# A gated delta-rule block on one core: the recurrence in two turns, joins on 128-row tiles, one PSUM pool

## The chip, the core and the metric

The kernel runs on one core of a Trainium2 chip. A core has five engines that work side by side and meet through semaphores: TensorE (matmuls, PE in the profile, with its weight loads as PEld), VectorE (DVE), ScalarE (ACT), GpSimd (POOL) and SyncE (SP), which here issues nearly all transfers (DMA). Each engine takes its instructions in the order in which they were laid down. Matmul results go to PSUM, which is used here as eight banks of 128 x 512 float32 values; everything else lies in SBUF, or in HBM when it doesn't fit. The metric is the time of one execution in microseconds. Before the change it is 4919.81 us, the median of three runs (4910.78 to 4920.14).

## The reference

Eight sequences of 512 tokens with 256 features go through one block: a normalized and modulated attention-like layer, and then a normalized and modulated feed-forward layer with experts. What matters here:

- Six modulation vectors come from a condition vector per sequence. Two of them, `ga` and `gb`, gate the two layers' results: `ga = (2*(ga >= 0) - 1) * max(|ga|, 0.25)`.
- The layer projects `h` to 16 key heads (q and k) and 32 value heads (v and z), each 128 wide. q, k and v go through a causal convolution of four taps and a SiLU. A key head serves two value heads: the kernel calls this a pair. Eight sequences by 16 pairs make 128 pairs.
- Per value head, the delta rule runs over chunks. In a chunk, `A = -(k_beta k^T * decay)` below the diagonal, `T = (I - A)^-1`, and with the state `S`:

```
v_new = T v_beta - (T (k_beta * exp(g))) S
out   = (q * exp(g)) S + tril(q k^T * decay) v_new
S     = S * exp(g_last) + (k * exp(g_last - g))^T v_new
```

- `out` is normalized, multiplied by the norm weights and by SiLU(z), and projected back to 256 features. The result, times `ga`, is added to x.
- A softmax over the mean of the tokens picks two of six experts per sequence; each is a 256-176-256 network with GELU. The weighted sum, times `gb`, is added to x.

## The kernel before, in words

The reference's chunks have 64 tokens; the kernel uses chunks of 128, which gives the same result: `NC = 4` chunks a sequence. One pair is the unit of work, and the main loop (L1075) is a software pipeline over 128 pairs. In iteration n these lists of steps are made and interleaved by `weave` (L52), which sorts all steps by their relative place in their own list; so the lists run side by side, each in its own order:

- `keys(n + LA)` with `LA = 9`: q and k of a pair nine ahead. Projection (L503), convolution (L511 on ScalarE, three L513 on VectorE), norms, the products k k^T and q k^T (L617), and the decay factors (L604, L610). The results wait in HBM (`kfar`, `qfar`, `sfar`, `m5far`, `m6far`, and the diagonal blocks in `lt`).
- one quarter of `diagonal_blocks(g)` for a group of four pairs: the inverses of the 32 x 32 diagonal blocks, by VectorE alone. A lane (partition) holds one block. Rows of 8 x 8 blocks come first, and then two joins: `join8_w`, `join8_x` and `join16_w`, `join16_x`, each a product (`mul`, such as L760 and L770) and a sum along the last axis (`red`). `minus_m` (L698) reads the matrix's block transposed.
- `join(n + 1)`: on TensorE, the 32-blocks are joined to 64 and those to 128, for eight matrices (u = 0..7: four chunks, two heads). Five steps follow one another: `w32` (L824) multiplies 128-row operands that hold two 32-blocks each, `x32` (L835) is a 32 x 32 product, `y32` (L846), `w64` (L857) and `y64` (L866) follow. Every step is eight matmuls into one PSUM bank, at output partitions that begin at 0, and then copies on ScalarE. The result is `y`, the transposed inverse.
- `values(n + 1)`: v of a pair one ahead (projection, convolution, SiLU), and `v_rows` (L890, L895), which turns them to rows.
- `recur(n)`: four chunks in a row. Per chunk, `from_state` (two matmuls `pi`, L919 and L920), `residual` (`r` on VectorE L927, `tmp` on ScalarE L932), `solve` (`u`, L941), `weigh` (`wd` on VectorE L950, `w` on ScalarE L956), `update` (`dst`, L964, and the new state on VectorE, L970 or L973), `within` (`in`, L982, `o` on VectorE, L988 or L990, and squares on ScalarE, L996). The state of one chunk is needed by the next: `pi`, `r`, `u`, `wd`, `dst`, `st` form a chain.
- `finish(n - 1)`: the norm (GpSimd), z's projection (`prz`, L1021), transposes (`ot`, L1044), the gate (`gt`, L1046), and the projection back (`op`, L1053), which is added to x.
- one side step where there is one: `before_attention` of the next sequence (L210), `after_attention` of the last one (L276: the experts), `gates` (L157).

After the steps of an iteration, the loads of the next pair's join are issued (L1110). SP issues the loads and stores in order; a load waits there until its buffer is free.

Matmuls in float32 make two records each in the profile, with a weight load each; transposes make one.

PSUM has three pools: `ps_m` with three banks (keys, values, side steps), `ps_c` with two (joins) and `ps_i` with three (recurrence and finish). A pool hands its banks out in turn, and a step that takes a bank waits for the last reader of what lay there.

`gates(b)` (L157) makes, once a sequence, 128 equal rows of the condition's SiLU, multiplies them with the weights (L166), and applies the sign and the limit of 0.25 in `sign_clip` (L147): one ScalarE copy and four VectorE instructions for each gate.

The diff touches these functions, and the main loop calls them:

Of the kernel before, what the change touches and what calls it, by code (L numbers as in the profile page):

```python
# [11 lines left out]
ALU = mybir.AluOpType  # L12
# [9 lines left out]
LA = 9  # L22
# [40 lines left out]
def adaln_block(  # L63
# [24 lines left out]
    ps_c = ctx.enter_context(tc.tile_pool(name="ps_c", bufs=2, space=PSUM))  # L88
    ps_i = ctx.enter_context(tc.tile_pool(name="ps_i", bufs=3, space=PSUM))
# [44 lines left out]
    wg6 = res.tile([P, 2, NKT, DM], F32, name="wg6")  # L134
# [12 lines left out]
    def sign_clip(dst, src, name):  # L147

        t = row.tile([P, DM], F32, name=f"sc_{name}", tag="scr", bufs=1)
        v = row.tile([P, DM], F32, name=f"sv_{name}", tag="sv", bufs=1)  # L150
        nc.scalar.copy(v, src)
        nc.vector.scalar_tensor_tensor(t, v, -1.0, v, ALU.mult, ALU.max)
        nc.vector.tensor_scalar_max(t, t, 0.25)
        nc.vector.tensor_scalar(v, v, 0.0, 2.0, ALU.is_ge, ALU.mult)
        nc.vector.scalar_tensor_tensor(dst, v, -1.0, t, ALU.add, ALU.mult)

    def gates(b):  # L157


        d = rows[b]  # L160
        sc = row.tile([P, NKT, P], F32, name=f"scr_{b}", tag="scr", bufs=1)
        nc.gpsimd.tensor_copy(sc, bc_last(silu_c[:, :, b], P))
        ps = bank(ps_m, f"gps_{b}")
        for i in range(2):
            for kt in range(NKT):
                mm(  # L166
                    ps[:, i * DM : (i + 1) * DM], sc[:, kt, :], wg6[:, i, kt, :],
                    start=kt == 0, stop=kt == NKT - 1,
                )
        for i, n in enumerate(("ga", "gb")):  # L170
            d[n] = row.tile([P, DM], F32, name=f"{n}_{b}", tag=n)
            sign_clip(d[n], ps[:, i * DM : (i + 1) * DM], f"{n}{b}")
# [37 lines left out]
    def before_attention(b):  # L210
# [63 lines left out]
        return [*norm_transposed(b, 0, 2, "a"), betas, lambda: (soft(), series()), decays]  # L274

    def after_attention(b):  # L276
# [75 lines left out]
        def hidden(t):  # L352
            if t == 0:
                f["hid"] = tiny("hid", [P, NF, SEQ])
            ps = bank(ps_m, f"f1_{b}_{t}")
            for kt in range(NKT):
                mm(  # L357
                    ps[: MF[t], :], f["s1"][:, kt, t * P : t * P + MF[t]], d["hb"][:, kt, :],
                    start=kt == 0, stop=kt == NKT - 1,
                )  # L360
            nc.scalar.activation(
                f["hid"][: MF[t], t, :], ps[: MF[t], :], AF.Gelu, bias=f["v1"][: MF[t], t : t + 1]
            )

        def result(i):
            ps = bank(ps_m, f"f2_{b}_{i}")
            for c2 in range(2):
                c = 2 * i + c2
                for t in range(NF):
                    mm(  # L370
                        ps[:, c2 * DM : (c2 + 1) * DM], f["hid"][: MF[t], t, c * P : (c + 1) * P],
# [14 lines left out]
            weigh, *[lambda t=t: hidden(t) for t in range(NF)],  # L386
            lambda: result(0), lambda: result(1),
# [3 lines left out]
    with tc.tile_pool(name="pro", bufs=1) as pro:  # L391
# [5 lines left out]
        )  # L397
        for i, col in enumerate((2 * DM, 5 * DM)):
# [19 lines left out]
        for i in (2, 6):  # L418
            nc.vector.tensor_scalar_add(modt[:, i : i + 2, :], modt[:, i : i + 2, :], 1.0)
        nc.scalar.activation(alog, alog, AF.Exp)  # L420
# [12 lines left out]
    with ExitStack() as st:  # L433
# [4 lines left out]
        keep = st.enter_context(tc.tile_pool(name="keep", bufs=LA + 3))  # L438
        far = st.enter_context(tc.tile_pool(name="far", bufs=LA + 3, space=DRAM))
# [7 lines left out]
        m5, x5, w5 = (w1b.tile([P, 8, 64], F32, name=n) for n in ("m5", "x5", "w5"))  # L447
        xw6 = w1b.tile([P, 8, 64], F32, name="xw6")
        x6, w6 = xw6[0:64], xw6[64:128]
        ysb = [w1b.tile([P, 8, P], F32, name=f"y_{i}") for i in range(2)]  # L450
        for t in (xl, yl, m5, x5, w5, xw6, *ysb):
            nc.gpsimd.memset(t, 0.0)
# [704 lines left out]
```

## Time and profile before

| what | value |
|---|---|
| median of three runs | 4919.81 us (4910.78 to 4920.14) |
| the profiled execution | 4912.86 us, its span 4911.1 us |
| TensorE busy, mean granted clock | 4569.8 us (93%), 0.965 |
| VectorE busy | 3815.8 us (78%) |
| ScalarE busy | 3120.0 us (64%) |
| GpSimd busy | 1826.3 us (37%) |
| DMA | 712.91 MB, 145 GB/s, q1 52.7% of 16 engines |
| first key projection, first recurrence | at 37.2 us, at 237.1 us |
| table loads of ScalarE for keys, values (L527) and decay (L610) | 140 and 121, 1283 ns each |

How to read it: the span is the time from the first to the last instruction of the program in one profiled execution; the run's time is a little longer. Busy time is the time in which at least one instruction of the engine runs. Matmuls overlap in their pipeline and their ends are modelled, so TensorE's busy share says little about how many results it delivers; the distance from one start to the next says more. A group of instructions is given with its line, engine, operation, output and inputs, sizes and count, then the busy time, the mean of one in ns, and after the second bar the idle time of the engine just before them, with what ended it.

### The profile page before, as it was taken

What the parts mean: (1) busy time and instruction counts of PE and PEld (TensorE: products, weight loads), DVE (VectorE), ACT (ScalarE), POOL (GpSimd) and SP (SyncE); (2) the same over time, 40 slices, a digit from 0 to 9 for tenths busy, and PEclk for the clock granted to TensorE, in tenths of its full rate; (3) what the DMA queues carried; (4) which work ended last, traced back from release to release, by engine and by line L of the source; (5) the groups of instructions that cost most, each with busy time, mean ns of one, the idle gap of its engine ahead of it and who ended that gap; (6) DMA issues with size and microseconds to landing.
All of it is one profiled execution on the core that took longest, in us unless ns stands there. A gap on an engine that the chain in (4) does not pass through costs nothing. (4 is left out here: it accounts for less than half of the span.)

```text
span 4911.1 us, 84235 instructions
## 1 busy us (share of the span) xinstructions
PE 4569.8 (93%) x27112; PEld 3262.1 (66%) x27112; DVE 3815.8 (78%) x8513; ACT 3120.0 (64%) x8899; POOL 1826.3 (37%) x1708
## 2 busy tenths in 40 slices
PE   5599999999999999999999999999999999999998
PEld 3366666666666666676666666666666666666775
DVE  4678878877878778888788887788877887878864
ACT  4566666666666666676666665666755666666553
POOL 3333434334333334334334343333333334333311
PEclk8689999999999999999999999999999999999998
DMA  5555555555555555555454555555555555556431
GB/s 154 120 142 146 145 160 150 155 145 155 151 144 155 150 151 143 141 157 159 150 158 143 146 163 147 144 157 146 160 138 145 149 151 154 140 148 158 133 107 46
DMA packets 1045671, 712.91 MB, mean 145 GB/s; under 512 B 661105, under 2 KB 909809, under 8 KB 1045233
## 3 DMA queue, kind: packets, MB, share of 16 engines
q1 hardware_dynamic: 1044416, 705.69, 52.7%
q8 instruction: 219, 3.59, 0.3%
q14 instruction: 220, 1.79, 0.1%
q10 hardware_dynamic: 816, 1.84, 0.1%
HBM read 459.27 MB, written 247.99 MB: 144 GB/s over the span
## 5 line engine op out<-in xcount | busy, mean ns | idle before, releaser
L513 DVE SCALAR_TENSOR_TENSOR cvv<-prv,cw,cvv 128x511 f32<-128x511 f32 (+2 forms) x768 | 560.5, 742 | 19.8 <-ACT cvv L511 18.3
L996 ACT ACTIVATE jo<-o 128x128 f32<-128x128 f32 x1024 | 304.5, 298 | 386.1 <-DVE o L990 350.9
L1031 POOL TENSOR_TENSOR msq<-msq,mhalf 128x8 f32<-128x8 f32 x128 | 223.3, 1744 | 876.6 <-DVE msq L1030 758.4
L1053 PE MATMUL op<-wo,gt 128*128 128x256 f32 x2048 | 504.9, 385 | 28.4 <-DVE gt L1046 21.8
L1021 PE MATMUL prz<-ha,wz 128*128 128x512 f32 x1024 | 496.7, 607 | 14.8 <-DMA wz<-in_dram 12.0
L637 POOL TENSOR_TENSOR mta<-mta,dca 128x512 f32<-128x512 f32 x256 | 326.3, 1275 | 466.6 <-DVE mta L626 429.4
L503 PE MATMUL prv<-ha,wv 128*128 128x512 f32 x1024 | 492.9, 603 | 4.9 <-DVE cvk L513 4.7
L604 ACT ACTIVATE dca<-gb,G 128x128 f32<-128x128 f32 x1024 | 334.8, 392 | 239.5 <-DMA sfar<-dca 179.8
L1053 PEld LDWEIGHTS op<-wo,gt 128*128 128x128 f32 x2048 | 370.6, 191 | 101.5 <-DVE gt L1046 37.4
L956 ACT ACTIVATE w<-u,br 128x128 f32<-128x128 f32 x1024 | 320.5, 361 | 164.3 <-DVE wd L950 130.0
L567 POOL TENSOR_TENSOR nrmk<-nrmk,half 128x4 f32<-128x4 f32 x128 | 140.9, 1101 | 741.3 <-ACT jk L563 727.5
L639 POOL TENSOR_TENSOR dca<-qkm,dca 128x256 f32<-128x256 f32 x512 | 387.6, 778 | 18.7 <-DVE qkm L631 0.6
L982 PEld LDWEIGHTS in<-w,s 128*128 128x128 f32 x2048 | 312.4, 197 | 92.7 <-issue 55.5
L982 PE MATMUL in<-w,s 128*128 128x128 f32 x2048 | 337.4, 287 | 4.3 <-ACT w L956 4.3
L617 PE MATMUL kk<-kqa 128*128 128x256 f32 x1024 | 314.2, 419 | 26.0 <-ACT kqa L527 14.6
L964 PE MATMUL dst<-wd,kr 128*128 128x256 f32 x768 | 265.7, 428 | 77.0 <-DVE wd L950 52.2
L513 DVE SCALAR_TENSOR_TENSOR cvk<-prk,cw,cvk 128x511 f32<-128x511 f32 (+2 forms) x384 | 285.8, 744 | 60.8 <-ACT cvk L511 57.8
L555 POOL TENSOR_TENSOR sq<-kqa 128x512 f32<-128x512 f32 x128 | 135.8, 1061 | 530.3 <-ACT kqa L527 530.3
L513 DVE SCALAR_TENSOR_TENSOR cvq<-prq,cw,cvq 128x511 f32<-128x511 f32 (+2 forms) x384 | 285.6, 744 | 40.6 <-ACT cvq L511 39.0
L503 PEld LDWEIGHTS prv<-ha,wv 128*128 128x128 f32 x1024 | 187.4, 192 | 182.8 <-issue 169.7
L941 PEld LDWEIGHTS u<-r,y 128*128 128x128 f32 x1536 | 235.7, 192 | 106.4 <-issue 51.9
L941 PE MATMUL u<-r,y 128*128 128x128 f32 x1536 | 291.2, 293 | 15.9 <-DVE r L927 15.1
(218 smaller groups left out, 11310.3 us busy)
## 6 DMA issues: line engine op xcount, KB each, us to landing
gb<-gfar SPq DMA_DIRECT2D x128, 512.0 KB
qfar<-kqa SPq DMA_DIRECT2D x128, 512.0 KB
kq<-qfar SPq DMA_DIRECT2D x128, 512.0 KB
sfar<-dca SPq DMA_DIRECT2D x256, 256.0 KB
s<-sfar SPq DMA_DIRECT2D x128, 512.0 KB
wk<-in_dram SPq DMA_DIRECT2D x256, 128.0 KB
wv<-in_dram SPq DMA_DIRECT2D x128, 256.0 KB
wz<-in_dram SPq DMA_DIRECT2D x128, 256.0 KB
```

Source lines behind the costliest of these rows:

```text
L503: mm(ps, d[wname][:, kt, j * P : (j + 1) * P], hT[:, kt, :], start=kt == 0, stop=kt == NKT - 1,)
L513: nc.vector.scalar_tensor_tensor(a[:, s:], ps[:, : SEQ - s], cw[:, ch, 3 - s : 4 - s], a[:, s:], ALU.mult, ALU.add,)
L604: nc.scalar.activation(dc[:, c, h, :], d["gb"][:, 2 * gr + c, h * P : (h + 1) * P], AF.Relu, bias=rw["G"][:, 2 * gr + c, k : k + 1], scale ...
L617: mm(ps[:, c2 * 2 * P : (c2 + 1) * 2 * P], d["kqa"][:, c, 0, :], d["kqa"][:, c].rearrange("p k i -> p (k i)"), start=True, stop=True,)
L637: nc.gpsimd.tensor_tensor(mt, mt, dc.rearrange("p c h i -> p (c h) i"), ALU.mult)
L639: nc.gpsimd.tensor_tensor(dc[:, c], bc_mid(d[f"qkm{gr}"][:, c, :], 2), dc[:, c], ALU.mult)
L941: mm(ps[:, h * P : (h + 1) * P], d["y"][:, 2 * c + h, :], r[:, h, :], start=True, stop=True,)
L956: nc.scalar.activation(w[:, h, :], ps[:, h * P : (h + 1) * P], AF.Copy, scale=d["br2"][:, c, h : h + 1],)
L982: mm(ps[:, h * P : (h + 1) * P], d["s"][:, 2 * c + h, :], cur["w"][:, h, :], start=True, stop=True,)
L996: nc.scalar.activation(junk, d["o"][:, c, h, :], AF.Square, accum_out=d["msq"][:, c, h : h + 1])
L1021: mm(ps, d["wz"][:, kt, h * P : (h + 1) * P], hT[:, kt, :], start=kt == 0, stop=kt == NKT - 1,)
L1053: mm(ps[:, k * DM : (k + 1) * DM], gt[h][:, c * P : (c + 1) * P], d["wo"][:, h, :], start=h == 0, stop=h == 1,)
```

## The change

The change has seven parts.

1. The recurrence takes two turns. `recur(n, 0)` does chunks 0 and 1 of pair n, and in the same iteration `recur(n - 1, 1)` does chunks 2 and 3 of the pair before. `finish` follows one iteration later, for pair n - 2. Values for `o`, `vr` and the loads of `kq`, `kr` and `s` are now kept in halves; the parts of `kq` and `kr` that are never used are no longer loaded. The gate's result is written over z.
2. Joins of two pairs go side by side: `join_w` multiplies the 32-join of the newer pair and the 64-join of the older one, in turn, and `join_y` ends both. All operands have 128 rows, with zeros where there is nothing, and one pair's results go to output partitions 0 to 63, the other's to 64 to 127 (in `join_y`, the product that was `x32` goes to 64 to 127). Their matmuls are laid down with high priority. Loads are issued in two parts: `join_diagonal` after an iteration, `join_corner` in `join_w`. There are four `y` tiles in place of two.
3. `ps_c` is gone; `ps_i` has five banks, for joins too.
4. The gates of all sequences are made once, in the prologue, on eight rows, and kept in HBM; `gates(b)` only loads them, spread to 128 partitions.
5. `LA` is 10 in place of 9. The five small tiles that a pair keeps until its turn are one tile, `kept`.
6. In `diagonal_blocks` the order of each join's two products is changed, so that no operand is read transposed.
7. The experts' hidden layer and result go by halves of 256 tokens; side steps of a sequence are put together (three steps before attention) and begin two iterations later.

```diff
-LA = 9
+LA = 10
...
-    ps_c = ctx.enter_context(tc.tile_pool(name="ps_c", bufs=2, space=PSUM))
-    ps_i = ctx.enter_context(tc.tile_pool(name="ps_i", bufs=3, space=PSUM))
+    ps_i = ctx.enter_context(tc.tile_pool(name="ps_i", bufs=5, space=PSUM))
...
     def gates(b):
-        d = rows[b]
-        sc = row.tile([P, NKT, P], F32, name=f"scr_{b}", tag="scr", bufs=1)
-        nc.gpsimd.tensor_copy(sc, bc_last(silu_c[:, :, b], P))
...
-            sign_clip(d[n], ps[:, i * DM : (i + 1) * DM], f"{n}{b}")
+        t = row.tile([P, 2 * DM], F32, name=f"gates_{b}", tag="gates")
+        nc.sync.dma_start(t, gates_far[b : b + 1, :].to_broadcast([P, 2 * DM]))
+        rows[b]["ga"], rows[b]["gb"] = t[:, :DM], t[:, DM:]
...
-            weigh, *[lambda t=t: hidden(t) for t in range(NF)],
-            lambda: result(0), lambda: result(1),
+            weigh, lambda: (hidden(0, 0), hidden(0, 1)), lambda: hidden(0, 2), lambda: result(0),
+            lambda: (hidden(1, 0), hidden(1, 1)), lambda: hidden(1, 2), lambda: result(1),
...
-            def join16_w(c, n, b):
-
-                pr = e["pr"].rearrange("p (c a b) -> p c a b", c=n, a=16)
+            def join16_w(a, n, w):
+
+                pr = e["pr"].rearrange("p (a b r) -> p a b r", a=n, b=16)
                 mul(
-                    pr, bc(minus_m(16, b, 16, 16 - b), 1, n), bc(part(yl, c, b, n, 16 - b), 2, 16),
+                    pr, bc(part(xl, 16 + a, 16, n, w), 2, 16), bc(part(e["t"], 0, 16, 16, w), 1, n),
                     ALU.mult,
                 )
...
+        def join_w(old, new):
+
+            p6 = bank(ps_i, f"w6_{old}") if old is not None else None
+            p5 = bank(ps_i, f"w5_{new}") if new is not None else None
+            with tc.high_priority(offset=1000):
+                for u in range(8):
+                    us = slice(64 * u, 64 * u + 64)
+                    if new is not None:
+                        mm(p5[:64, us], m5[:, u, :], x5[:, u, :], start=True, stop=True)
+                    if old is not None:
+                        mm(p6[64:, us], m6[:, u, :], x6[:, u, :], start=True, stop=True)
+            if old is not None:
+                nc.scalar.copy(w6[64:128], of_u(p6, 64)[64:128])
+            if new is not None:
+                v = of_u(p5, 64)
                 nc.scalar.copy(w5[32:64, :, 0:32], v[0:32, :, 0:32])
                 nc.scalar.copy(w5[96:128, :, 32:64], v[32:64, :, 32:64])
+                join_corner(new)
+
+        def join_y(old, new):
...
+            with tc.high_priority(offset=1000):
                 for u in range(8):
+                    us = slice(64 * u, 64 * u + 64)
+                    if new is not None:
+                        mm(p5[:64, us], w5[:, u, :], halves(y5[:, u, :]), start=True, stop=True)
+                        mm(
+                            p5[64:, 32 * u : 32 * u + 32], y5[:, u, 0:64], w5[:, u, 0:32],
+                            start=True, stop=True,
+                        )
+                    if old is not None:
+                        mm(p6[:64, us], w6[:, u, :], y6[:, u, 64:128], start=True, stop=True)
+            if old is not None:
+                nc.scalar.copy(y6[0:64, :, 64:128], of_u(p6, 64)[0:64])
+            if new is not None:
+                v = of_u(p5, 64)
+                nc.scalar.copy(x6[32:64, :, 0:32], of_u(p5, 32)[96:128])
+                nc.scalar.copy(y5[0:32, :, 32:64], v[0:32, :, 0:32])
+                nc.scalar.copy(y5[64:96, :, 96:128], v[32:64, :, 32:64])
...
-            for c in range(NC):
+            for c in (2 * half, 2 * half + 1):
                 if c:
                     steps.append(lambda c=c: from_state(c))
                     steps.append(lambda c=c: residual(c))
...
-                gt[h] = w1b.tile([P, SEQ], F32, name=f"gt{h}_{n}", tag=f"gt{h}")
+                gt[h] = d[f"z{h}"]
...
             if 0 <= m <= last:
-                sj = loaded.pop(m)
-                load, sv = values(m)
-                load()
-                streams += [sj, sv]
+                load_half(m, 0)
+                streams.append(values(m))
             if 0 <= n <= last:
-                streams.append(recur(n))
-            if 0 < n:
-                streams.append(finish(n - 1))
+                load_half(n, 1)
+            old = m if 0 <= m <= last else None
+            new = m + 1 if 0 <= m + 1 <= last else None
+            if old is not None or new is not None:
+                streams.append([
+                    lambda old=old, new=new: join_w(old, new), lambda old=old, new=new: join_y(old, new),
+                ])
+            if 0 <= n <= last:
+                streams.append(recur(n, 0))
+            if 0 <= n - 1 <= last:
+                streams.append(recur(n - 1, 1))
+            if 0 <= n - 2 <= last:
+                streams.append(finish(n - 2))
             weave(*streams, side.pop(n, []))
-            if 0 <= m + 1 <= last:
-                lj, loaded[m + 1] = join(m + 1)
-                lj[0]()
-            its.pop(n - 1, None)
+            if 0 <= m + 2 <= last:
+                join_diagonal(m + 2)
+            its.pop(n - 2, None)
```

## The prediction

> **What bounds the kernel now.** I read the page's first part, then busy time by stretch, then TensorE's timeline inside one steady pair of heads, then the groups by line. The page first:
>
> ```profile
> span 4911.1 us, 84235 instructions
> PE 4569.8 (93%) x27112; PEld 3262.1 (66%) x27112; DVE 3815.8 (78%) x8513; ACT 3120.0 (64%) x8899; POOL 1826.3 (37%) x1708
> ```
>
> By stretch (columns: stretch, length, then busy time of PE, PEld, DVE, ACT, POOL, granted clock, DMA share, GB/s): from the first `u` of pair 0 (237 us) to that of pair 118 (4585) every pair also makes keys; from there to 4844 the last pairs run without key work.
>
> ```profile
> 237.00:4585.00 4348.00, 4135.30 (x24855) 2960.18 (x24855) 3495.47 (x7787) 2848.20 (x8181) 1675.48 (x1551) 0.98 0.55 150
> 4585.00:4844.00 259.00, 254.88 (x1672) 188.63 (x1671) 171.52 (x348) 139.81 (x417) 54.26 (x45) 0.99 0.36 103
> ```
>
> TensorE leads (95% busy), VectorE follows (80%), ScalarE has 66%, DMA 55%. A full pair takes 4348/118 = 36.85 us, one without keys 259/9 = 28.8. VectorE is busy 3495/118 = 29.6 us a pair: a floor that cannot be far undercut. A busy PE is not a PE at its peak, so the timeline matters more (start, length, line, tiles, count, idle before):
>
> ```profile
> 2517.58 1.88 PE L503 MATMUL prv<-ha,wv 128*128 128x512 f32 x4
> 2519.30 1.88 PE L503 MATMUL prq<-ha,wk 128*128 128x512 f32 x4
> 2521.11 1.15 PE L824 MATMUL w<-x,m 128*64 128x64 f32 x16
> 2522.18 0.70 PE L964 MATMUL dst<-wd,kr 128*128 128x256 f32 x2
> ...
> 2526.81 0.70 PE L919 MATMUL pi<-st,kq 128*128 128x256 f32 x2 [1.77 <-DVE st L970]
> ...
> 2529.23 0.33 PE L846 MATMUL py<-y,w 128*64 128x64 f32 x2
> 2529.69 0.49 PE L941 MATMUL u<-r,y 128*128 128x128 f32 x2
> 2530.11 0.33 PE L846 MATMUL py<-y,w 128*64 128x64 f32 x2
> 2530.36 0.49 PE L941 MATMUL u<-r,y 128*128 128x128 f32 x2
> 2530.78 0.91 PE L846 MATMUL py<-y,w 128*64 128x64 f32 x12
> ```
>
> Four 512-wide records go from 2517.58 to 2519.30: 0.43 us each. The next four should end at 2521.02, yet the join (`w`, 64 columns) starts at 2521.11: 0.09 late, with no wait named. Start-to-start medians of the same records over 500 to 4500 us say it for all: 429 ns for 512 columns, 216 for 256, 112 for 128, 58 for a 64-column join, 32 for `px`; but 522, 309 and 205 where the next one is a join, and 151 after a join's last one. So each edge between a join and a full-width matmul costs 93 ns, both ways. Joins are broken up (`py`, `u`, `py`, `u`, `py` above): in the built TensorE order they stand in 1147 runs, 9.0 a pair. That is 2 x 1147 x 0.093 = 213 us. Busy time hides nearly all of it.
>
> The other loss is the recurrence (`pi` waits 1.77 us for the state above). Idle before its groups:
>
> ```profile
> L941 PE MATMUL u<-r,y 128*128 128x128 f32 x1536 | 291.2, 293 | 15.9 <-DVE r L927 15.1
> L964 PE MATMUL dst<-wd,kr 128*128 128x256 f32 x768 | 265.7, 428 | 77.0 <-DVE wd L950 52.2 <-DVE rk L581 16.3 <-DVE gt L1046 4.5
> L919 PE MATMUL pi<-st,kq 128*128 128x256 f32 x768 | 248.9, 406 | 39.5 <-DVE st L970 34.2 <-DVE prl L721 4.3 <-DVE yl L722 0.9
> ```
>
> With `in` (4.3) that is 137 us. After such a wait the second record comes 0.1 us late too: (start-to-start) some 500 records of these lines in 4000 us, 56 us, 69 over the span. Together 206 us.
>
> [...] No join of before leaves column 0[...]; the waits for `st` and `wd` fit a chain too short of other work, and don't single out banks.
>
> **The change part by part.** The sum is made against the profiled span, 4911.1 us (its run took 4912.9; the median of the runs shown is 4919.8, so the span plus 8).
>
> *Join edges.* Two joins of different pairs now go together, in two blocks a pair: 271 runs in the built order. 876 runs fewer x 2 x 0.093 = **-163**. Nothing hides this; TensorE is the leader.
>
> *Join matmuls.* Still 40 a pair (80 records, 10,240 in all), now all on 128 rows, alternating between output columns 0-63 and 64-127. If the two halves don't overlap, 64-column records stay at 58 ns, and the former `px` (32 ns, 32-column weights) loads 64 columns: 2048 x 26 ns = +53 at worst. If they overlap fully, some 30 ns each: (64 x 58 + 16 x 32 - 80 x 30) ns x 128 = -233. I take 64-column records at 46 ns: 8192 x 12 ns = **-100**. The seven ScalarE copies (0.35 to 0.58 us each) stay seven; between the blocks the built order has some 9 us of other matmuls to hide them.
>
> *Recurrence in two turns.* Chunks 0 and 1 of one pair run beside chunks 2 and 3 of the pair before. Matmul time between the ends of a link, from the built orders with the durations above, on average: `pi` to `u` 2.3 us before and 5.3 after; `u` to `dst` 2.7 and 4.8; `u` to `in` 3.6 and 6.7; `dst` to next `pi` 2.1 and 4.4. In the undisturbed tail one link takes about 1.2 us (`u` at 4843.75, `wd` at 4844.51, `dst` at 4844.97), the rest is queueing on VectorE. Twice the cover should take half of 206: **-110** (bounds -40 and -170). Five shared banks for 24 tiles a pair, instead of three for 20 and two for five, belong here; a join holds two at once, from its matmuls to its copies.
>
> *Gates once.* 64 records (16.1 us) and eight two-fold sign/clip chains leave; `dst` and key weights wait some 16 us on them. Instead: one small product at the start and a DMA of 256 KB per batch, an iteration ahead: **-30** (bounds -10, -40).
>
> *Diagonal blocks.* Operands are read along rows. The forms compared:
>
> ```profile
> L760 DVE TENSOR_TENSOR prl<-tl,yl 128x1024 f32<-128x1024 f32 x96 | 186.0, 1938 | 0.0
> L770 DVE TENSOR_TENSOR prl<-xl,wt 128x1024 f32<-128x1024 f32 x96 | 117.2, 1221 | 0.3
> ```
>
> If all take the second form's time, 96 x 0.717 = 69 us leave VectorE; the 512-wide pair (1045 against 711 ns, 64 times) 21 more, the gates 22. These 112 us lie beside TensorE's work; what they give is fewer late results: **-20** (bounds 0, -50).
>
> *Depth.* LA is 10 and a pair finishes one iteration later. A key-only iteration takes 17 to 20 us at the start (`prk` at 37.20, 54.48, 74.30, 94.27): +20; one pair moves from 36.85 to 28.8: -8; half a recurrence in an iteration of its own at the end, whose matmuls are few: +12. **+24**.
>
> *FFN halves, loads in halves.* FFN columns are as many as before. SP gets 393 more issues; at 0.5 us that is 1.5 us a pair, SP being 48% busy. They come an iteration ahead of use, and behind them stand key and value weights, loaded as early; without that cover up to 1.5 us a pair. `kq` and `kr` loads shrink by 192 KB a pair. ScalarE has 28 more table loads x 1.283 = 36 us, at 66% busy: **+5** together.
>
> *Given back.* These sum to -394, or 3.1 us of 36.85 a pair. VectorE, 29.6 - 0.9 = 28.7 us, would then be 85% busy, and its queue is in order: results come later again. I give back **+45**. Span 4911 - 349 = 4562; with 8 on top **4570 us**.
>
> **Rivals.**
>
> *A, only the edges pay.* Halves don't overlap, VectorE's queue eats the shorter waits: -163 + 53 - 40 - 30 + 24 + 5 = -151: 4770 us. For it: a weight load of 128 columns with a one-column matmul (`ssq`) also takes 112 ns, so loads may set the pace. Against: doubled cover.
>
> *B, all of it.* -163 - 233 - 170 - 30 - 50 + 24 + 5 = -617: about 4300; VectorE would then be 28.7/32.0 = 90% busy, so rather 4350. For it: PE reached 98% busy in the last pairs, where VectorE has 66%.
>
> *C, slower[...].* If moving between columns 0 and 64 costs what a change of shape costs, 93 ns: 16 changes in each of two blocks x 128 = 4096 x 0.093 = +381, over -163 - 110 - 30 - 20 + 24 + 5 = -294: span 4998, **5006 us**. It decides from 294/4096 = 0.072 us a change. [...] for it: no trace of before has the change.
>
> **How the numbers follow.** The forecast 0.60 (its own range 4460 to 4690), A 0.19 (4690 to 4840), B 0.11 (4310 to 4460), C 0.08, no change 0.02. Runs of before spread by 0.2%, so 0.2% is what can be told from nothing. 4400 to 4810 holds all of the forecast, most of A and half of B: 0.8. Faster 0.90, within 0.2% 0.02, slower 0.08.
>
> **What would show it.** Edges: 522 and 205 ns become rare, about 540 edges in all. Overlap: a join block's 32 records take about 1.5 us (1.9 without, over 3 with C), the 48-record block about 2.0. Waits: idle before `dst`, `pi`, `u` falls to half. VectorE: 1938 becomes about 1221, its share of the span 81%. Full pairs at about 34 us. First `u` near 257 us. I am wrong if join records come slower than 58 ns, or if TensorE's idle before `dst` and `pi` doesn't fall.

## The result and the profile after

The changed kernel takes 4841.66 us (median of four runs, 4832.29 to 4857.62), beside 4915.43 us for the kernel before in the same set (4910.78 to 4920.14): ratio 0.9843 [0.9812, 0.9874]. That is faster, by 74 us where 350 were forecast, 152 us above the forecast's own range (4460 to 4690) and 32 us above the wider one (4400 to 4810). The profiled execution took 4833.8 us. Its page begins:

```profile
span 4832.1 us, 85394 instructions
PE 4206.3 (87%) x27152; PEld 3058.3 (63%) x27152; DVE 3664.4 (76%) x8453; ACT 3173.5 (66%) x8936; POOL 1827.3 (38%) x1704
```

By stretch, with the columns of the forecast's first table (from the first `u` of pair 0 to that of pair 118, and from there to the last pair's):

```profile
250.60:4534.50 4283.90, 3787.45 (x24822) 2762.41 (x24821) 3341.25 (x7703) 2890.67 (x8184) 1669.19 (x1540) 0.96 0.56 147
4534.50:4755.90 221.40, 218.61 (x1604) 168.34 (x1604) 156.26 (x327) 136.36 (x404) 44.96 (x36) 1.00 0.38 105
```

Against before, the start costs 13.6 us, the 118 full pairs give 64.1, the nine last pairs 37.6, and the end costs 9.1: 79.0 us of span. The last pairs are the key to the case. They make no keys, and fell from 28.8 to 24.6 us each; that is 4.2 us, more than the forecast's 3.1. The full pairs fell by only half a microsecond, to 36.3. TensorE's busy time is 364 us lower, the span only 79: most of what was saved turned into waiting.

The groups of TensorE that wait (busy time, mean ns; after the second bar idle time before them, and what ended it); first the two of before that the prediction doesn't show, then those of after:

```profile
L503 PE MATMUL prv<-ha,wv 128*128 128x512 f32 x1024 | 492.9, 603 | 4.9 <-DVE cvk L513 4.7
L547 PE MATMUL kt<-ident,kqa 128*128 128x128 f32 x512 | 101.0, 296 | 42.5 <-ACT kqa L527 37.2 <-DVE cvq L513 5.0
```

```profile
L963 PE MATMUL u<-r,y 128*128 128x128 f32 x1536 | 268.5, 284 | 13.3 <-DVE r L949 10.8 <-DMA y<-ly 1.3 <-DVE ix L280 1.1
L986 PE MATMUL dst<-wd,kr 128*128 128x256 f32 x768 | 258.4, 421 | 84.0 <-DVE wd L972 37.6 <-issue 31.4 <-DVE yl L723 4.5
L941 PE MATMUL pi<-st,kq 128*128 128x256 f32 x768 | 251.2, 411 | 3.2 <-DVE yl L723 3.1
L502 PE MATMUL prv<-ha,wv 128*128 128x512 f32 x1024 | 517.4, 631 | 146.0 <-DVE cvk L512 128.4 <-ACT w L978 17.2
L546 PE MATMUL kt<-ident,kqa 128*128 128x128 f32 x512 | 95.3, 317 | 189.5 <-DVE cvq L512 78.1 <-DVE prl L722 69.8 <-ACT kqa L526 39.4
```

The recurrence's own waits did fall: `pi` from 39.5 to 3.2 us, `u` from 15.9 to 13.3. Two groups that the forecast never looked at took their place: `prv` (projection of v) and `kt` (transposes of the finished k).

### One pair, taken apart

From 500 to 4400 us I split a pair's period (start to start of `prk`) into TensorE's idle time, the time lost to a lowered clock (TensorE's busy time in each stretch of the record of the granted clock, times one minus the clock), and the rest, which is work at full clock. In us:

| kernel | period | idle | lost to the clock | work |
|---|---|---|---|---|
| before | 36.84 | 1.83 | 0.66 | 34.35 |
| after | 36.53 | 4.21 | 1.28 | 31.04 |
| decay factors behind q (below) | 34.99 | 2.91 | 0.88 | 31.20 |
| the same, no inverses of diagonal blocks (below) | 33.89 | 2.11 | 0.44 | 31.34 |

Work fell by 3.31 us a pair, more than the forecast's 3.1 for all its terms. Idle time took back 2.38 and the clock 0.62: 3.00 x 118 = 354 us net, where the forecast gave back 45. The question is what TensorE waits for.

### The loop

The chain of waits inside one pair, from one `kt` to the next (start, length, what; in order of time):

```profile
2499.63 0.64 PE kt L546 x3
...
2506.58 1.73 PE prz L1043 x4
...
2508.33 2.52 DMA wz<-in_dram
...
2512.18 1.72 POOL dca L644 x2
...
2518.76 1.96 POOL dca L644 x2
2520.74 2.10 DMA sfar<-dca
...
2522.92 0.40 ACT dca L609
...
2526.75 0.66 DVE cvk L512
...
2535.67 0.67 DVE cvq L512
...
2536.47 1.10 PE kt L546 x4
```

From the end of one `kt` (2500.27) to the end of the next (2537.57) it takes 37.3 us; the mean period of a pair is 36.5. To be read as a loop: GpSimd multiplies the key products by the decay factors (`mta`, `dca`). The store `sfar` must be done before ScalarE may write the next pair's decay factors into the same two buffers (`dca`, L609). ScalarE takes its instructions in order (in this pair it stood idle from 2528.39 to 2529.70 us with q's projection complete from 2527.77, then did the SiLU of k with its table load, and only at 2531.53 `cvq`), and behind `dca` stands the convolution of k (`cvk`, L510); behind that, on VectorE, the rest of the convolutions of k and q. On TensorE `prv` needs the PSUM bank that `cvk` reads. `kt` reads only k, but it too takes a bank of this pool, and it starts here at 2536.47, as soon as the last `cvq` has read q's projection and before the SiLU of q is done:

```profile
2536.42 0.63 ACT L526 ACTIVATE kqa<-cvq 128x512 f32<-128x512 f32 x1 [2.14 <-DVE cvq L512]
```

So both waits appear to be for banks that late convolutions have yet to read (e2 below bears this out). TensorE is in order too (in the trace of e14, below, every place of its order holds the same instruction as in e6, while e14 takes 43 us longer): `dst`, `pi` and `prz` stand behind `kt` whether they need keys or not. (In this pair the link back to GpSimd runs through a load of `wz` that waited for `prz`; most often it is `mta` on VectorE, which ended 377.9 of the 536.7 us that GpSimd idles before its first product.) ScalarE shows the same wait, in the group of its decay factors before the change and after it:

```profile
L604 ACT ACTIVATE dca<-gb,G 128x128 f32<-128x128 f32 x1024 | 334.8, 392 | 239.5 <-DMA sfar<-dca 179.8 <-issue 36.5 <-POOL mta L637 19.2
```

```profile
L609 ACT ACTIVATE dca<-gb,G 128x128 f32<-128x128 f32 x1024 | 333.7, 390 | 413.2 <-DMA sfar<-dca 270.0 <-issue 112.3 <-POOL nrm L581 12.1
```

And here is TensorE's timeline of the changed kernel at the end of that pair:

```profile
2529.78 1.95 PE L502 MATMUL prv<-ha,wv 128*128 128x512 f32 x4 [0.71 <-DVE cvk L512]
2531.58 0.38 PE L963 MATMUL u<-r,y 128*128 128x128 f32 x2
2531.80 0.60 PE L986 MATMUL dst<-wd,kr 128*128 128x256 f32 x2
2532.23 0.61 PE L1004 MATMUL in<-w,s 128*128 128x128 f32 x4
2536.47 1.09 PE L546 MATMUL kt<-ident,kqa 128*128 128x128 f32 x4 [3.63 <-DVE cvq L512]
2537.41 1.19 PE L986 MATMUL dst<-wd,kr 128*128 128x256 f32 x2
```

It is idle for 3.63 us before `kt`, and then runs at half clock: `dst` takes 1.19 us where 5.6 us earlier it took 0.60. The record of the granted clock has 0.5 for 3.4 us from 2536.2. From 500 to 4400 us there are 33 stretches at half clock before the change and 68 after it, and 1 and 37 gaps of over 3 us in TensorE's work. Each of these gaps has a stretch of its own that begins in it or within 3.5 us of its end; what brought the other 32 and 31 is not shown. At half clock for 3.4 us, this wait costs by my estimate up to 1.7 us (half of 3.4) on top of its 3.63.

### The profile page after: what moved, and what is told of

Its sections match the earlier page's. It is cut to its first block, busy times and chain, and to the rows that moved or that the text cites. A ratio compares the mean times of both kernels' runs of the same rounds, so it can differ in the third digit from the quotient of the medians.

```text
span 4832.1 us, 85394 instructions
## 1 busy us (share of the span) xinstructions
PE 4206.3 (87%) x27152; PEld 3058.3 (63%) x27152; DVE 3664.4 (76%) x8453; ACT 3173.5 (66%) x8936; POOL 1827.3 (38%) x1704
## 4 chain that ended last, share of the span: by engine, by line
PE 24%; DVE 15%; DMA 11%; POOL 10%; ACT 8%; issue 4%; SPq 3%; POOLq 0%; DVEq 0%; ACTq 0%
PE prz L1043 5%; POOL dca L644 4%; POOL mta L642 3%; DMA tl<-lt 3%; DMA sfar<-dca 3%; PE prv L502 2%; DVE cvk L512 2%; PE op L1075 2%; ACT dca L609 2%; POOL nrm L581 2%; PE pi L941 2%; PE dst L986 1%; ACT jo L1018 1%; PE pi L942 1%; DVE mta L631 1%
## 5 line engine op out<-in xcount | busy, mean ns | idle before, releaser
L502 PE MATMUL prv<-ha,wv 128*128 128x512 f32 x1024 | 517.4, 631 | 146.0 <-DVE cvk L512 128.4
L609 ACT ACTIVATE dca<-gb,G 128x128 f32<-128x128 f32 x1024 | 333.7, 390 | 413.2 <-DMA sfar<-dca 270.0
L512 DVE SCALAR_TENSOR_TENSOR cvv<-prv,cw,cvv 128x510 f32<-128x510 f32 (+2 forms) x768 | 567.4, 740 | 23.5 <-ACT cvv L510 21.5
L642 POOL TENSOR_TENSOR mta<-mta,dca 128x512 f32<-128x512 f32 x256 | 332.1, 1297 | 536.7 <-DVE mta L631 377.9
L1075 PE MATMUL op<-wo,z 128*128 128x256 f32 x2048 | 489.9, 381 | 7.4 <-DVE z L1068 6.2
L978 ACT ACTIVATE w<-u,kept 128x128 f32<-128x128 f32 x1024 | 322.0, 366 | 168.6 <-DVE wd L972 117.9
L644 POOL TENSOR_TENSOR dca<-qkm,dca 128x256 f32<-128x256 f32 x512 | 413.1, 827 | 22.7 <-DVE prl L722 3.4
L1075 PEld LDWEIGHTS op<-wo,z 128*128 128x128 f32 x2048 | 375.6, 190 | 64.0 <-DVE z L1068 14.9
L954 ACT ACTIVATE tmp<-pi,kept 128x128 f32<-128x128 f32 x768 | 237.7, 362 | 184.8 <-DVE r L949 166.4
L1061 POOL TENSOR_TENSOR wo<-wo,gates 128x512 f32<-128x512 f32 x128 | 178.9, 1398 | 443.3 <-DMA wo<-in_dram 363.5
L986 PE MATMUL dst<-wd,kr 128*128 128x256 f32 x768 | 258.4, 421 | 84.0 <-DVE wd L972 37.6
L1004 PE MATMUL in<-w,s 128*128 128x128 f32 x2048 | 313.1, 276 | 0.9 <-DVE prl L722 0.9
L622 PE MATMUL kk<-kqa 128*128 128x256 f32 x1024 | 285.4, 401 | 22.5 <-ACT kqa L526 18.0
L512 DVE SCALAR_TENSOR_TENSOR cvk<-prk,cw,cvk 128x511 f32<-128x511 f32 (+2 forms) x384 | 284.5, 741 | 19.2 <-ACT cvk L510 17.6
```

The source lines that it names most:

```text
L502: mm(ps, d[wname][:, kt, j * P : (j + 1) * P], hT[:, kt, :], start=kt == 0, stop=kt == NKT - 1,)
L512: nc.vector.scalar_tensor_tensor(a[:, s:], ps[:, : SEQ - s], cw[:, ch, 3 - s : 4 - s], a[:, s:], ALU.mult, ALU.add,)
L609: nc.scalar.activation(dc[:, c, h, :], d["gb"][:, 2 * gr + c, h * P : (h + 1) * P], AF.Relu, bias=rw["G"][:, 2 * gr + c, k : k + 1], scale ...
L622: mm(ps[:, c2 * 2 * P : (c2 + 1) * 2 * P], d["kqa"][:, c, 0, :], d["kqa"][:, c].rearrange("p k i -> p (k i)"), start=True, stop=True,)
L642: nc.gpsimd.tensor_tensor(mt, mt, dc.rearrange("p c h i -> p (c h) i"), ALU.mult)
L644: nc.gpsimd.tensor_tensor(dc[:, c], bc_mid(d[f"qkm{gr}"][:, c, :], 2), dc[:, c], ALU.mult)
```

## The experiments

All ratios are to the kernel before in the same set, with 95% intervals; "after" is the changed kernel. Sets differ a little from one another, so a difference between two kernels in us is that of their ratios times 4915 us.

### Is it the loop?

The expectations call the loop theory L. Theory B is that the three banks of `ps_m` set the pace, theory V that VectorE is full.

**e6_dca_after_q.** One tiny VectorE instruction makes the bias of the decay factors from the finished q (times zero). ScalarE then has `dca` after both key convolutions. Nothing else moves by design, but other instructions do change places in the traces, on TensorE too. The same edit was made in the kernel before (e6b).

```diff
+                gk = sm.tile([P, NC, 2], F32, name=f"gk_{n}", tag="gk")
+                nc.vector.scalar_tensor_tensor(
+                    gk, bc_last(d["kqa"][:, :, 1, 0], 2), 0.0, rw["G"][:, :, hs], ALU.mult, ALU.add
+                )
...
-                                bias=rw["G"][:, 2 * gr + c, k : k + 1], scale=-1.0,
+                                bias=gk[:, 2 * gr + c, h : h + 1], scale=-1.0,
```

> The changed kernel; one small VectorE instruction per pair (about 0.2 us) makes the decay factors' bias from G and zero times the finished q, so that ScalarE can take a pair's decay factors only after both its key convolutions. Four buffers for dca did not take the wait away, because the built order then put the decay factors of one pair further ahead in front of the same convolution. Theory L: ScalarE's idle before dca falls under 200 us (413), TensorE's idle before prv and kt under 170 together (335), time 4640 to 4750 us. Rivals (VectorE's queue in front of the q convolution, or the order of TensorE): 4800 to 4880 us.

4686.8 us, ratio 0.9551 [0.9532, 0.9570]: 144 us faster than after. ScalarE's wait is gone, and TensorE's two waits fell with it (a new one came up: the joins' `py` waits 91.7 us, nearly all of it ended by the gate on VectorE, `z`, where it waited 1.0 before):

```profile
L613 ACT ACTIVATE dca<-gb,gk 128x128 f32<-128x128 f32 x1024 | 313.4, 404 | 8.1 <-DVE gk L605 4.3 <-DMA sfar<-dca 3.3 <-DMA lt<-mta 0.3
```

```profile
L502 PE MATMUL prv<-ha,wv 128*128 128x512 f32 x1024 | 486.6, 599 | 26.2 <-ACT w L982 13.6 <-DVE cvk L512 9.4 <-DVE prl L726 3.2
L546 PE MATMUL kt<-ident,kqa 128*128 128x128 f32 x512 | 85.3, 292 | 77.0 <-DVE cvq L512 49.7 <-ACT kqa L526 24.4 <-DVE yl L727 2.8
```

> The same edit in the kernel before. Theory L (the loop only became the bound when TensorE's work shrank): 4880 to 4940 us, within 0.7% of before. If it gains over 1.5%, the loop was a bound before the change too.

5192.74 us, ratio 1.0576 [1.0558, 1.0594]. In the kernel before, the same edit costs 5.8%, far outside what was expected. ScalarE's wait before `dca` goes there too (239.5 to 11.4 us), but `ot` waits 138.4 us in place of 10.1, and `kk` and `vt` wait longer by 42 and 61. So the edit is no gift in itself. Why it costs that much there was not found.

**e13_pool_more, e14_q_pool_more.** The loop is made longer: two GpSimd multiplications by one, some 0.8 us each (the products of this shape, L639, took 778 ns in the mean before), ahead of a pair's second store; in after, and in e6.

```diff
+                if gr == 1:
+                    for c in range(2):
+                        nc.gpsimd.tensor_tensor(dc[:, c], dc[:, c], bc_mid(ones, 2), ALU.mult)
```

> The changed kernel with the loop made longer and nothing else: GpSimd multiplies a pair's second half of the decay products by one (two instructions of about 0.8 us) before they are stored. GpSimd is 38% busy. Theory L (products on GpSimd, store, the next pair's decay factors on ScalarE, and behind them its key convolution, set the pace): up to 1.6 us more a pair, 4950 to 5050 us. If the pace is set elsewhere, 4830 to 4880 us.

> The same two GpSimd instructions in the kernel whose decay factors come after both key convolutions (4687 us). Theory L: the store no longer stands before a convolution, so at most 0.4 us a pair come through: 4680 to 4740 us. If GpSimd's queue as such is the pace, 4800 us or more.

5013.6 us, ratio 1.0174 [1.0149, 1.0199], and 4745.87 us, 0.9639 [0.9615, 0.9663]. GpSimd is busy for 38% of the span, yet in after its extra 1.6 us a pair cost 163 us, or 1.27 us a pair; with `dca` behind q they cost 43 us, 0.34 a pair (the time itself came a little above what was expected). The order of instructions hardly moves here: in the traces 97 to 99% of the places on TensorE, ScalarE and VectorE hold the same instruction in e13 as in after, and all of them in e14 as in e6. This is the most direct evidence for the loop: work on an engine that is mostly idle is paid to four fifths, until the loop is loosened.

**e1_dca4, e5_before_dca4.** Four buffers for `dca` in place of two, in after and in before.

```diff
-                    dc = d[f"dca{gr}"] = w2b.tile([P, 2, 2, P], F32, name=f"dca_{n}_{gr}", tag="dca")
+                    dc = d[f"dca{gr}"] = w2b.tile([P, 2, 2, P], F32, name=f"dca_{n}_{gr}", tag="dca", bufs=4)
```

> The changed kernel with four buffers for the decay factors (dca) in place of two. Theory L (a loop through the key work sets the pace: the decay factors of the next pair wait on ScalarE until the stores of this pair have freed dca, and the next pair's key convolution stands behind them in ScalarE's order): ScalarE's idle time before dca falls from 413 us to under 150, TensorE's idle before prv and kt (146 and 189 us) to under 170 together, time 4640 to 4740 us. Theory B (the three PSUM banks of ps_m, for which prv waits, set the pace): within 0.5% of 4842. Theory V (VectorE is full): within 0.5% of 4842.

> The kernel before with four buffers for dca in place of two. Theory L says that before the change TensorE's own work was as long as the loop (36.85 us a pair), so that freeing dca gives little: 4830 to 4915 us. If it gives as much as in the changed kernel (over 2%), the loop was the bound all along and the change removed nothing that mattered.

4856.61 us, 0.9863 [0.9832, 0.9894], and 5124.54 us, 1.0424 [1.0391, 1.0457]. By its number the first run came out as theories B and V expected, and the second came out worse than any branch. But this was no clean way to take the wait away. The order of instructions is built from the dependencies: with more buffers free, the decay factors of a pair are laid down earlier (before the convolution of the preceding pair's k), and wait for the store there; in after, ScalarE's idle time before them is then 571 us (353 of them ended by the store) in place of 413 (270). So e1 says nothing against the loop, since the wait grew. What made e5 slower was not found.

### What else holds TensorE

**e2_psm4.** `prv` waits for a bank that `cvk` reads, so keys and values get a fourth bank from the other pool.

```diff
-    ps_m = ctx.enter_context(tc.tile_pool(name="ps_m", bufs=3, space=PSUM))
-    ps_i = ctx.enter_context(tc.tile_pool(name="ps_i", bufs=5, space=PSUM))
+    ps_m = ctx.enter_context(tc.tile_pool(name="ps_m", bufs=4, space=PSUM))
+    ps_i = ctx.enter_context(tc.tile_pool(name="ps_i", bufs=4, space=PSUM))
```

> The changed kernel with four banks in ps_m and four in ps_i, in place of three and five. Theory B (prv waits for a bank that the key convolution frees late, and everything behind it on TensorE waits along): idle before prv falls from 146 us to under 30 and the time to 4700 to 4760 us. Theory L (the loop through dca): prv's wait goes, but reappears before kt, which stands a few matmuls later in the same order: 4810 to 4870 us.

4811.77 us, 0.9785 [0.9756, 0.9813], 29 us faster than after. From 500 to 4400 us the wait of `prv` is gone (133.5 in after) and that of `kt` fell from 135 to 30 us, so both had been for banks; but `in` and `kk` wait in their place (85 and 55 us, where they had under 1), and `dst` still waits 74. ScalarE still idles 259 us before `dca`. A fourth bank for the keys is one fewer for the rest, so the run prices the exchange, not the bank alone.

**e4_no_diag, e15_q_no_diag.** VectorE's work on the inverses of the 32 x 32 diagonal blocks is left out but for its first instructions, its load and its stores; in after, and in e6.

```diff
-                [begin, *[lambda i=i: row(i) for i in range(1, 8)], turn8],
-                [lambda: join8_w(0), lambda: join8_w(1), lambda: join8_x(0), lambda: join8_x(1)],
...
+                [begin, lambda: row(1)],
+                [],
+                [],
+                [leave],
```

> The changed kernel without VectorE's work on the 32 x 32 diagonal blocks, but for the first row's copy (so the wait for the load of tl stays) and the stores; the inverses are left out of the computation. About 6 us of VectorE's 29 us a pair go. Theory V (VectorE's queue, with that work in front of the key convolutions, sets the pace): 4200 to 4450 us, and TensorE's busy share over 95%. Theory L: the loop keeps its other parts (GpSimd, store, ScalarE): 4600 to 4780 us.

> The kernel after with the decay factors behind q's convolution (4687 us), and VectorE's work on the inverses of the diagonal blocks left out (the result is then not the reference's). Leaving that work out alone gave 177 us, the delayed decay factors alone 155. If both remove the same wait (the key convolutions' results come late, by ScalarE's queue or by VectorE's), they don't add: 4610 to 4680, TensorE idle 2.4 to 2.9 us a pair. If VectorE's load is a bound of its own, they add: 4500 to 4540.

4664.31 us, 0.9497 [0.9476, 0.9517], and 4528.07 us, 0.9195 [0.9178, 0.9212]. It takes 5.4 us a pair off VectorE (28.4 to 23.0 us). Alone it gives 170 us (theory V expected over 390), on top of e6 another 175: the two add. So VectorE's load is a second holder in its own right. That fits the row of `kt` above, where 69.8 us of idle time ended with a product of these inverses (`prl`), and what is left of the waits in e15:

```profile
L502 PE MATMUL prv<-ha,wv 128*128 128x512 f32 x1024 | 484.4, 597 | 20.7 <-ACT w L979 20.7
L987 PE MATMUL dst<-wd,kr 128*128 128x256 f32 x768 | 235.7, 389 | 3.4 <-DVE wd L973 1.0 <-ACT v L526 1.0 <-ACT kqa L526 0.3
L546 PE MATMUL kt<-ident,kqa 128*128 128x128 f32 x512 | 84.4, 290 | 39.7 <-ACT kqa L526 27.9 <-DVE cvq L512 8.0 <-DVE cvv L512 2.5
```

Loop and load together are worth 318 us; with both out of the way the time is 4528 us, below the forecast (though with less to compute). That bounds what VectorE holds; it doesn't say which of its results come late, since a fifth of its work is gone.

**e11_q_psm4, e18_q_psi6, e19_q_pools.** e6 with its eight banks shared out otherwise: four and four; two for keys and values and six for the rest; three for keys and values, two for joins alone, three for recurrence and finish.

> The kernel after with the decay factors behind q's convolution (4687 us), and four banks for ps_m, four for ps_i. If what is left of TensorE's idle time are waits for a bank of keys and values: 4620 to 4660. If they are waits for VectorE whatever the bank: 4670 to 4710.

> The kernel after with the decay factors behind q's convolution (4687 us), with six banks in the one pool and two in ps_m. If the pool of joins, recurrence and finish is short of banks: 4560 to 4650. If two banks for keys and values are the tighter place: over 4740.

> The kernel after with the decay factors behind q's convolution (4687 us), with two banks for joins alone and three for recurrence and finish. If joins and recurrence stand in each other's banks, as in the rest of the change without joins and turns: 4580 to 4650. If two half recurrences and finish need the five banks: over 4740.

4826.38 us (0.9804 [0.9788, 0.9821]), 4875.48 us (0.9901 [0.9879, 0.9923]), 4887.95 us (0.9930 [0.9905, 0.9956]): each is 124 to 186 us slower than e6. e18 and e19 came out in their upper branch; e11 came out above both of its branches. The kernel is slower with more banks and with fewer in the shared pool alike. The number of banks also changes the built order of all engines, so these runs don't tell a shortage of banks from a worse order. One comparison limits what e6 shows: e11 is e2 with the edit of e6, and there the edit gains nothing (0.9785 to 0.9804), although ScalarE's idle time before `dca` fell from 259 to 23 us. Another wait took over: `ot` waits 182 us in e11, 14 in e2. So the 144 us are what the edit gives with three and five banks, and not the price of the loop wherever it stands.

### The parts of the change

**e7_one_turn, e9_old_joins, e12_rest.** After with all four chunks of a pair in one turn; with the five joins of before; with both.

```diff
             if 0 <= n <= last:
-                streams.append(recur(n, 0))
-            if 0 <= n - 1 <= last:
-                streams.append(recur(n - 1, 1))
+                streams.append(recur(n, 0) + recur(n, 1))
```

```diff
-                    lambda old=old, new=new: join_w(old, new), lambda old=old, new=new: join_y(old, new),
...
+                streams.append(loaded.pop(m))
```

> The changed kernel with all four chunks of a pair in one turn, as before; everything else as changed (finish still one iteration later). Theory L: the recurrence isn't what ends last, so the time stays within 1% of 4842. If the two turns are what the change gains by, TensorE's idle before dst and pi comes back to over 110 us and the time is 4880 to 4980 us.

> The changed kernel with the joins of before (five steps a pair, all at output column 0, 644 runs in the built TensorE order in place of 271), drawn from the five-bank pool. In the changed kernel's trace a pair's join records take 2.9 us in place of 4.2, and each edge costs 93 ns. If TensorE's work is what ends last, the old joins cost 128 x 1.3 + 2 x 373 x 0.093 = 236 us: 5050 to 5100 us. If the pace is set elsewhere (L or V), TensorE's idle time shrinks by as much and the time is 4820 to 4930 us.

> The changed kernel with the old joins and with the recurrence in one turn: what is left of the change is the one PSUM pool, LA = 10, the gates, the diagonal blocks' order of products, FFN and loads by halves. If the parts add up (joins 181 us, turns 144 us, both measured by undoing them), 5130 to 5200 us, which makes the rest a loss of over 200 us. If undoing either already brings the same stalls, 4980 to 5080 us.

4985.73 us (1.0130 [1.0103, 1.0158]), 5022.95 us (1.0230 [1.0212, 1.0247]), 5048.13 us (1.0244 [1.0218, 1.0269]). Undoing the turns costs 141 us, undoing the joins 190, undoing both only 197, so the two gains don't add. In e7 the recurrence waits again: from 500 to 4400 us 145 us before `u`, 83 before `pi` (11 and 0.5 in after). Theory L expected a time within 1% of after and was wrong there: the loop isn't the only thing that can hold TensorE. In e9 TensorE's work at full clock is 2.1 us a pair more than in after, or 251 us over 118 pairs, and the time rises by less, to between the two branches expected. Both parts work; but what remains of the change without them is 2.4% slower than the kernel before.

**e16_rest_q, e17_rest_pools.** Why? e12 with the edit of e6, and e12 with the two joins' banks and three of the kernel before.

> The rest of the change without new joins and turns (5048 us), with the decay factors behind q's convolution. If the loop through the key products, the store and the decay factors is what makes the rest slower than the kernel before: 4870 to 4960. If not, no gain or a loss as in the kernel before (there the edit cost 5.8%): 5040 to 5300.

> The rest of the change without new joins and turns (5048 us), with the old pools: two banks for joins, three for recurrence and finish. If the one pool is what makes the rest slower than the kernel before (joins and recurrence in each other's banks): 4900 to 4960. If the pool helps or doesn't matter: 5030 to 5150.

4931.85 us (1.0025 [1.0013, 1.0037]) and 4948.29 us (1.0061 [1.0041, 1.0081]). Each alone brings back most of the 2.4%: e6's edit 2.2, the pools 1.8. With the old pools the recurrence's waits are what fell (`pi` 84.7 to 28.6 us, `u` 54.3 to 11.4). That would fit joins and recurrence in each other's banks, but e16, which keeps the one pool, has them at 16.6 and 14.3; so it isn't shown. In the full change with e6's edit, e19, the old pools cost time. Whether loop and pool add in the rest was not run.

### A better kernel

**e10_q_wo.** e6, with the output weights loaded an iteration earlier.

```diff
+        def out_load(n):
+            p = n % HK
             wo = its[n]["wo"] = wp.tile([P, 2, DM], F32, name=f"wo_{n}", tag="wo")
...
+            if 0 <= n - 1 <= last:
+                out_load(n - 1)
```

> The kernel whose decay factors come after both key convolutions, with the load of the output weights an iteration earlier, so that GpSimd doesn't wait for it (354 us) with the next products behind. If that wait is a part of what is left, 4600 to 4660 us; if it is only idle time of an engine with slack, within 0.5% of 4687.

4670.3 us, 0.9473 [0.9447, 0.9499]: 0.8% under e6 by the ratios, 0.4% by the medians. GpSimd's wait for these weights fell from 354 to 137 us. By its time the run falls into the branch of an engine with slack; the wait is a small part of what is left, if any. It is the fastest kernel here that computes the whole, 5.3% faster than before and 3.8% faster than after (0.9473/0.9843); most of the latter is e6's edit.

## Why the prediction was wrong

The sign was right, the size was not, and the step that failed is **"Given back"**: +45 us for VectorE's in-order queue, a term set down without a working. By the split of a pair 354 us were given back. The runs put two things in its place: the loop through the key products, their store and ScalarE's decay factors (144 us, e6), which no step of the forecast names, and VectorE's load (175 more, e15), which it names and under-sized. That the loop holds TensorE in after is shown (e13, e6); its 144 us hold for this sharing of the banks only (e11). The profile of before had the loop in it: ScalarE's 239.5 us of idle time before `dca`, ended by the store. The prediction prices ScalarE by its busy share (66%) and has no term for its idle time. At 36.8 us a pair that did no harm: `prv` and `kt` waited 4.9 and 42.5 us in all. A period of 34 needed that loop to turn faster, and no part of the change was made for it.

The other steps, one by one:

- **Join edges, -163.** The trace has the 271 runs, and an edge still costs 93 ns (112 and 205 ns between starts without and with one). The count of before was a little high: its trace has the joins in 1021 runs, and the other 126 of the 1147 are changes from one form of join to another inside a run, so some -151 was due. No run parts this term from the next.
- **Join matmuls, -100 (bounds +53 and -233).** The mechanism was right and the term mis-sized: the halves overlap fully, and the records of a pair took 2.9 us in place of 4.2, some -170. Starts in TensorE's timeline of after, with one product for each half in turn:

```profile
2528.03 0.22 PE L835 MATMUL w<-x,m 128*64 128x64 f32 x1
2528.04 0.22 PE L837 MATMUL w<-x,m 128*64 128x64 f32 x1
2528.09 0.22 PE L835 MATMUL w<-x,m 128*64 128x64 f32 x1
```

  A record of the other half starts 7 ns later by the trace's finer times, and a pair of them every 59 ns, so 32 records take 0.95 us; the forecast said 1.5. The block of 48 takes 1.9 us, near its 2.0, since 32 of its records go to one half; that is why the far bound of -233 wasn't reached. Rival C falls with this, and so does A's first assumption.
- **Recurrence in two turns, -110.** `pi`'s idle time fell as forecast, and e7 puts the turns at 141 us. But `dst` rose from 77.0 to 84.0, so that all four groups together fell from 137 to 101 us and not to half. In e6, `dst` waits 17.6 and all four 19: that part of the term, too, was held back by late results. The failed part is its count of cover: only for links of the recurrence. By the built orders, the matmuls between `prq` and `kt` fell from 6.1 to 4.4 us, and nobody counted those.
- **Gates -30, depth +24, loads and tables +5.** Not tested apart. The first `u` came at 250.6 us (257 forecast), the end costs 9.1 us (12 forecast). e12 shows that the rest of the change, these terms among it, loses 2.4%, some 120 us, where they were summed as a gain of 21 with the diagonal blocks. The one PSUM pool is part of that rest too; the prediction had it under the recurrence's gain.
- **Diagonal blocks, -20.** VectorE lost 151 us of busy time (112 forecast). The two large products took part in that with less than forecast; of after:

```profile
L762 DVE TENSOR_TENSOR prl<-xl,tl 128x1024 f32<-128x1024 f32 x96 | 130.9, 1363 | 0.0
L773 DVE TENSOR_TENSOR prl<-wt,yl 128x1024 f32<-128x1024 f32 x96 | 134.1, 1397 | 0.4
```

  Their means 1938 and 1221 ns became 1363 and 1397, 38 us in all and not 69. The form itself does what was forecast: the median of each is 1.22 us. But 53 of the 192 took 1.3 to 2.2 us, and during these GpSimd was busy for 90% of the time in the first group and 61% in the second, against 33 and 29% during the others. No run tests whether that is the cause.

Rival A's figure (4770) was nearest, by luck for the most part: it has halves that don't overlap and a recurrence that gains little, and only its late results from VectorE's queue are in the runs. Here TensorE's saving came in full and was then mostly waited away.

## What to carry to other kernels

When the leading engine gets shorter, look for the next loop before pricing the gain: follow a buffer that is written anew each round through its store, its writer and what is queued behind that writer, and compare its length with the new period. Count the cover of every wait on the leader's queue, not only of those that the change is about. And where instructions are ordered by a scheduler, more buffers or banks are not a neutral test: they move the order, so look for the wait itself in the run before judging. Adding work to an idle engine of the suspected loop left the order as it was, and made the cleaner test.

## What the runs showed of the hardware

Two things I had not expected. Column halves of 64 run side by side in float32, weight loads included: 59 ns for a record of each, the 58 ns that a 64-column record took alone before. All of them use all 128 rows, and each record has a weight load of its own; one of the second half's loads starts at 2528.041 us while a product of the first half runs (2528.032 to 2528.254 in the trace, which models the ends). And idle time came with a surcharge: in after, 4.21 us of idle time a pair came with 1.28 us lost to the half clock, in e15 2.11 with 0.44.
